# The second tile's products ahead of the third tile's transposes, in the maps of the mean and in the last projection

## Chip, cores and metric

The kernel runs on one core of one Trainium2 chip. The metric is device microseconds for one execution. The kernel before takes 3393.33 us, the median of three runs (3391.39 to 3394.57).

## What is computed

Four graph layers follow one another on 3327 nodes with 512 features, all with the same adjacency matrix. Each layer's output is added to its input and normalised row by row:

```python
x = _layernorm(x + _L0_gnn_ref(x, adj, W, a))                 # attention, 8 heads of 64
x = _layernorm(x + _L1_gnn_ref(x, adj, W_nb, b_nb, W_line, b_line, 64))  # mean of up to 64 neighbours
x = _layernorm(x + _L2_gnn_ref(x, adj, W, a))                 # attention, 8 heads of 64, then elu
x = _layernorm(x + _L3_gnn_ref(x, adj, W, a))                 # attention, 4 heads of 128, then elu
```

The mean layer maps the mean of a node's neighbours with `W_nb`, and the node itself with `W_line`; each map has a bias and a leaky relu, and the two are added. An attention layer begins with a projection, `Wh = x @ W`, from which the scores of the heads are taken as well:

```python
Wh = (h @ W).reshape(n, H, D)
s1 = jnp.einsum('nhd,hd->nh', Wh, a1)
s2 = jnp.einsum('nhd,hd->nh', Wh, a2)
```

## The kernel before

The 3327 rows are padded to 26 tiles of 128 (`NT`). The stages follow one another: projection and attention of layer 0; the maps of the mean (first part of `sage`, lines 712 to 775), that is both linear maps applied to the rows of layer 0; the sums over the kept neighbours together with the projection of layer 2 (second part of `sage`); attention of layer 2; the projection of layer 3 (first part of `third`, lines 897 to 942); attention of layer 3 and the output.

The two stages that are edited have the same form. A tile's row of work is:

- *Finish* the layer before (`finish`, `finish_steps`, `norm_rows`), two tiles at a time. The attention's sums `h` are loaded from memory, and the residual rows `xr` with them; VectorE divides (L181) and adds (L197, or L194 and L195 around an exponential L186 on ScalarE), takes statistics (L152, L153), ScalarE takes the root (L154), VectorE the reciprocal and the shift (L155, L158), and ScalarE normalises the rows in place (L161).
- *Transpose* the tile: four TensorE transposes into PSUM (L724 in `step1`, L261 in `project1`) and one copy to SBUF on ScalarE, `xT` (L726, L262). In the last projection VectorE sums `xT` as well (L263).
- *Products* of the transposed tile. In the maps these are `step2`: four matmuls with `wn` into `pz` (L732), four with `wl` into `pi` (L735). The profile lists each of these fp32 matmuls as two, so a tile has 16. ScalarE casts `pz` to bf16 (L736), VectorE subtracts (L738), ScalarE casts the remainder (L739), VectorE makes the third piece (L741) and finishes the map of the node itself (L744, L745, L746); two stores go out on SP's queue (L742, L747). In the last projection they are `project2`: eight matmuls of 260 columns into two banks (L271, 16 in the profile), an exponential (L272) and two small copies (L275) on ScalarE, two multiplications on VectorE (L277), and one store on SP (L283).

The loop runs one tile behind itself: the products of a tile are kept in `pend` and issued after the transposes of the next tile, so that the copy of the transposed tile is covered. For tiles 0, 1, 2 the order on TensorE is thus transposes 0, transposes 1, products 0, transposes 2, products 1, transposes 3, products 2. Tiles 0 and 1 (`first`) were already finished by the stage before; the loop handles two tiles in each pass (`t0`), and asks for the next two when it has transposed the first of a pair.

What sets the order: `tc.manual_schedule` at the top keeps TensorE in the order in which the program issues its instructions. The other engines' instructions are put in order by the scheduler, except those that are marked `keep_in_program_order`. Each engine works through its own queue in that order. PSUM tiles of the stage (`pt`, and `pz`, `pi`, or the two banks `pw`) have two buffers each. In the last projection, after the products of tile 13, `prepare` transposes the scores of the first half (L312), copies them (L314) and stores them; thirteen small transposes in groups of four share two PSUM buffers.

Of the kernel before, what the change touches and what calls it, by code (L numbers as in the profile page):

```python
# [32 lines left out]
def kernel(  # L33
# [94 lines left out]
    def store_tile(dst, src, t, eng):  # L128
        if dst.shape[0] == N and t == NT - 1 and LAST < P:
            for a, z in _row_pieces(LAST):  # L130
                eng.dma_start(out=dst[t * P + a:t * P + z, :], in_=src[a:z, :])
        else:
            eng.dma_start(out=dst[t * P:(t + 1) * P, :], in_=src)

    def load_w(pool, src, name, eng=None):
        t = pool.tile([P, FC, src.shape[1]], F32, name=name)
        (eng or nc.scalar).dma_start(out=t, in_=src.rearrange("(c p) m -> p c m", p=P))
        return t


    def load_wide(t, src, eng):
        for e in range(2):
            eng.dma_start(out=t[:, :, e, :FW], in_=src[:, e * FW:(e + 1) * FW].rearrange("(c p) m -> p c m", p=P))
# [61 lines left out]
    def finish(*a):  # L205
        ys, steps = finish_steps(*a)
        for f in steps:
            f()
        return ys
# [476 lines left out]
    def sage(first, first_pool, xin, prev, nxt, wsrc, dst):  # L686
# [3 lines left out]
        with tc.tile_pool(name="sg_z", bufs=1, reuse_waits="tile") as zp, \  # L690
# [17 lines left out]
            def zs(t, c):  # L708
                return zs_[t // HALF][:, t % HALF, c, :]

            zd = dram.tile([NP, F], BF, name="zd")
            with tc.tile_pool(name="sa_w", bufs=1, reuse_waits="tile") as wp, \
                    tc.tile_pool(name="sa", bufs=2, reuse_waits="tile") as fp, \
                    tc.tile_pool(name="sa_t", bufs=2, reuse_waits="tile") as sp, \
                    tc.tile_pool(name="sa_ps", bufs=2, space=PSUM, reuse_waits="tile") as ps:
                wn = load_w(wp, wnT, "wn", nc.gpsimd)
                wl = load_w(wp, wlT, "wl", nc.gpsimd)
                blb = wp.tile([P, F], F32, name="blb")
                nc.gpsimd.dma_start(out=blb, in_=bl.to_broadcast([P, F]))

                def step1(xt):
                    pt = ps.tile([P, FC, P], F32, name="pt")
                    for c in range(FC):
                        nc.tensor.transpose(pt[:, c, :], xt[:, c * P:(c + 1) * P], ident)  # L724
                    xT = sp.tile([P, FC, P], F32, name="xT")
                    nc.scalar.copy(xT, pt)  # L726
                    return xT

                def step2(xt, xT, t):
                    pz = ps.tile([P, F], F32, name="pz")  # L730
                    for c in range(FC):
                        nc.tensor.matmul(pz, xT[:, c, :], wn[:, c, :], start=c == 0, stop=c == FC - 1)  # L732
                    pi = ps.tile([P, F], F32, name="pi")
                    for c in range(FC):
                        nc.tensor.matmul(pi, xT[:, c, :], wl[:, c, :], start=c == 0, stop=c == FC - 1)  # L735
                    nc.scalar.copy(zs(t, 0), pz)  # L736
                    r1 = sp.tile([P, F], F32, name="r1")
                    nc.vector.tensor_tensor(r1, pz, zs(t, 0), op=ALU.subtract)  # L738
                    nc.scalar.copy(zs(t, 1), r1)  # L739
                    z3 = sp.tile([P, F], BF, name="z3")  # L740
                    nc.vector.tensor_tensor(z3, r1, zs(t, 1), op=ALU.subtract)  # L741
                    nc.sync.dma_start(out=zd[t * P:(t + 1) * P, :], in_=z3)  # L742
                    xi = sp.tile([P, F], F32, name="xi")
                    nc.vector.tensor_tensor(xi, pi, blb, op=ALU.add)  # L744
                    nc.vector.scalar_tensor_tensor(xi, xi, 0.01, xi, op0=ALU.mult, op1=ALU.max)  # L745
                    nc.vector.tensor_tensor(xi, xi, xt, op=ALU.add)  # L746
                    nc.sync.dma_start(out=xid[t * P:(t + 1) * P, :], in_=xi)  # L747


                cr = fp.tile([NT, P], BF, name="cr", bufs=1)  # L750
                nc.sync.dma_start(out=cr, in_=ctd[NT:NT + 1, :].rearrange("o (t p) -> (o t) p", p=P))
                cnt = zp.tile([P, 3, NT], F32, name="cnt")
                pend = None
                ahead = first
                for t0 in range(0, NT, 2):
                    ys = ahead
                    if t0 in (4, 8):
                        prev.late.pop(0)(fp)
                    if t0 == 8:
                        cf = fp.tile([NT, P], F32, name="cf", bufs=1)  # L760
                        nc.scalar.copy(cf, cr)
                        pt = ps.tile([P, FC, P], F32, name="pt")
                        cb = pt[:, 0, :NT]
                        nc.tensor.transpose(cb, cf, ident[:NT, :NT])
                        nc.vector.tensor_scalar(cnt[:, 0, :], cb, NEIGHBOURS, 1.0, op0=ALU.min, op1=ALU.max)
                        nc.vector.reciprocal(cnt[:, 1, :], cnt[:, 0, :])
                        nc.vector.tensor_scalar(cnt[:, 2, :], cb, 0.0, None, op0=ALU.is_gt)
                    for s, y in enumerate(ys):
                        xT = step1(y)
                        if s == 0 and t0 + 2 < NT:  # L770
                            ahead = finish(fp, xin, prev, t0 + 2, 2, 6, nc.sync if t0 else nc.gpsimd)
                        if pend:
                            step2(*pend)
                        pend = (y, xT, t0 + s)
                step2(*pend)
            first_pool.close()

            with tc.tile_pool(name="sb_w", bufs=1, reuse_waits="tile") as wp, \
# [8 lines left out]
                wsb = wp.tile([P, FC, 2, FW + nxt.H], F32, name="wsb")  # L787
# [60 lines left out]
                for b in range(len(blocks)):  # L848
                    t0, i0 = blocks[b]
# [42 lines left out]
    def third(first):  # L892
        with tc.tile_pool(name="col3", bufs=1) as cp, tc.tile_pool(name="at_r3", bufs=2, reuse_waits="tile") as rp:
# [3 lines left out]
            with tc.tile_pool(name="p_w", bufs=1, reuse_waits="tile") as wp, \  # L897
                    tc.tile_pool(name="p", bufs=3, reuse_waits="tile") as pp, \
                    tc.tile_pool(name="p_f", bufs=2, reuse_waits="tile") as fp, \
                    tc.tile_pool(name="p_ps", bufs=2, space=PSUM, reuse_waits="tile") as ps:  # L900
                wsb = wp.tile([P, FC, 2, FW + L3.H], F32, name="wsb")

                def bank(e):
                    return ps.tile([P, 512], F32, name=f"pw{e}")


                pend = None
                ahead = first
                groups = []

                def load_group(t0):
                    if t0 < NT:
                        groups.append(finish_steps(fp, x2, L2, t0, 2, 10, nc.gpsimd if t0 < 4 else nc.sync, 6,
                                                    pinned=t0 == 2))
                        groups[-1][1].pop(0)()

                load_group(2)
                load_wide(wsb, w3, nc.gpsimd)
                nc.vector.tensor_copy(wsb[:, :, :, FW:], wa[3].rearrange("p c (e h) -> p c e h", e=2))
                load_group(4)  # L920
                for t0 in range(0, NT, 2):
                    ys = ahead
                    if t0 in (4, 8):
                        L2.late.pop(0)(fp)
                    load_group(t0 + 6)
                    for s, y in enumerate(ys):
                        t = t0 + s
                        store_tile(x3, y, t, nc.sync)
                        xT = L3.project1(pp, ps, y, t)
                        if s == 0 and groups:  # L930
                            ahead, steps = groups.pop(0)
                            for f in steps:
                                f()
                        if pend:
                            L3.project2(pp, bank, wsb, *pend)
                        pend = (xT, t)
                        if t == HALF + 1:
                            L3.prepare(pp, 0)
                            L3.first_rows = L3.rows(rp, 0, 0)
                            L3.cut(pp, 0)  # L940
                L3.project2(pp, bank, wsb, *pend)
                L3.mean(pp, bank, wsb)

# [129 lines left out]
    L0, L2, L3 = Layer(0, 8, False), Layer(2, 8, True), Layer(3, 4, True)  # L1073
# [3 lines left out]
    with tc.tile_pool(name="col0", bufs=1) as cp, tc.tile_pool(name="raw", bufs=2) as rawp, \  # L1077
# [4 lines left out]
        with tc.tile_pool(name="p_w", bufs=1, reuse_waits="tile") as wp, \  # L1082
# [37 lines left out]
            wsb = wp.tile([P, FC, 2, FW + L0.H], F32, name="wsb")  # L1120
# [3 lines left out]
            pend = (xT, 0)  # L1124
            for t in range(1, NT):
                xT = L0.project1(pp, ps, load(t), t)
                L0.project2(pp, bank, wsb, *pend)
                pend = (xT, t)
# [96 lines left out]
```

## Time and profile before

| | us |
|---|---|
| median of three runs | 3393.33 |
| the profiled execution | 3389.15 |
| its span | 3387.4 |
| TensorE busy | 3251.2 |
| VectorE busy | 2687.5 |
| ScalarE busy | 2354.6 |
| maps of the mean: first transposes of a tile to the last product | 960.2 to 1168.2 |
| last projection: first transposes to the last product | 2555.9 to 2684.1 |

The mean granted clock of TensorE was 0.985 of full speed.

How to read the lines shown below. PE is TensorE's matmuls, PEld its weight loads, DVE VectorE, ACT ScalarE, POOL GpSimd, SP SyncE. In the timeline, each line gives the start and the duration in us, the engine, the line of the program, the operation, what it writes and reads, how many instructions are merged, and in brackets how long the engine had been idle before and which instruction released it. A line of the waits says who waited for whom, in us in total, how often, and the longest. A line of the stretches gives its bounds and length in us; then the busy time and the number of instructions of PE, PEld, DVE, ACT and POOL; then the granted clock, the DMA share and GB/s.

### The profile page before, as it was taken

What the parts mean: (1) busy time and instruction counts of PE and PEld (TensorE: products, weight loads), DVE (VectorE), ACT (ScalarE), POOL (GpSimd) and SP (SyncE); (2) the same over time, 40 slices, a digit from 0 to 9 for tenths busy, and PEclk for the clock granted to TensorE, in tenths of its full rate; (3) what the DMA queues carried; (4) which work ended last, traced back from release to release, by engine and by line L of the source; (5) the groups of instructions that cost most, each with busy time, mean ns of one, the idle gap of its engine ahead of it and who ended that gap; (6) DMA issues with size and microseconds to landing.
All of it is one profiled execution on the core that took longest, in us unless ns stands there. A gap on an engine that the chain in (4) does not pass through costs nothing.

```text
span 3387.4 us, 47182 instructions
## 1 busy us (share of the span) xinstructions
PE 3251.2 (96%) x18476; PEld 1626.4 (48%) x18476; DVE 2687.5 (79%) x2619; ACT 2354.6 (70%) x2143; POOL 239.8 (7%) x389
## 2 busy tenths in 40 slices
PE   8899999999979999999989999999998999999997
PEld 7634344444434445545544444444446754455453
DVE  5799999999967544444449999999998766668887
ACT  2398998999953333333338999999997655558986
POOL 3100000000010011111110000000002000010110
PEclk9999999999999999999999999999998999999998
DMA  9644111110143343333320111111117411122211
GB/s 368 222 124 127 49 49 38 55 49 28 44 123 125 122 117 84 91 85 87 80 77 20 47 48 50 51 48 47 35 31 241 152 41 42 41 51 80 94 42 49
DMA packets 288014, 284.29 MB, mean 84 GB/s; under 512 B 107492, under 2 KB 223534, under 8 KB 287791
## 3 DMA queue, kind: packets, MB, share of 16 engines
q1 hardware_dynamic: 254063, 170.62, 16.6%
q0 software_dynamic: 28208, 102.96, 9.5%
q10 hardware_dynamic: 5520, 7.69, 0.7%
q8 instruction: 146, 2.39, 0.3%
q14 instruction: 77, 0.63, 0.1%
HBM read 212.01 MB, written 69.17 MB: 83 GB/s over the span
## 4 chain that ended last, share of the span: by engine, by line
PE 85%; DVE 5%; DMA 4%; ACT 3%; issue 2%; SPq 0%; ACTq 0%; DVEq 0%; POOL 0%; POOLq 0%
PE po L428 52%; PE acc L859 12%; PE pd L380 7%; PE pw L271 5%; DVE t L405 3%; PE pz L732 3%; DMA raw<-in_adjT_dram 3%; PE pi L735 3%; ACT y L408 1%; PE pt L456 1%; PE pk L819 1%; DMA h<-hd 0%; PE pa L1108 0%; PE pt L724 0%; PE pct L664 0%
## 5 line engine op out<-in xcount | busy, mean ns | idle before, releaser
L405 DVE SCALAR_TENSOR_TENSOR t<-rb,qc,mask 128x1664 f32<-128x1664 f32 x1040 | 1960.3, 1954 | 169.4 <-PE po L428 147.3
L408 ACT ACTIVATE y<-t,bi,sc 128x1664 fp8e4<-128x1664 f32 x1040 | 1769.5, 1766 | 310.4 <-PE pd L380 292.7
L428 PE MATMUL po<-t,vj 128*64 128x448 f32 (+3 forms) x8320 | 1909.6, 521 | 22.1 <-DVE t L405 19.6
L428 PEld LDWEIGHTS po<-t,vj 128*64 128x64 f32 (+1 forms) x8320 | 838.9, 148 | 970.6 <-issue 704.0
L859 PE MATMUL acc<-zs,kt 128*128 128x512 bf16 x1352 | 401.1, 380 | 0.0
L271 PE MATMUL pw<-wsb,xT 128*128 128x264 f32 (+1 forms) x1248 | 302.2, 397 | 15.2 <-DVE vt L277 12.0
L859 PEld LDWEIGHTS <-kt 128*128 128x128 fp8e4 x2002 | 196.1, 98 | 242.1 <-issue 7.7
L811 ACT CAST pk<-cy 128x512 f32<-128x512 bf16 x169 | 99.0, 588 | 277.4 <-DVE kt L823 266.3
L271 PEld LDWEIGHTS pw<-wsb,xT 128*128 128x128 f32 x1248 | 241.1, 197 | 60.7 <-ACT xT L262 10.8
L380 PE MATMUL pd<-y,sden 128*32 128x448 fp8e4 (+1 forms) x4160 | 259.5, 342 | 10.4 <-ACT y L408 10.4
L859 PE MATMUL acc<-zl,kt 128*128 128x512 bf16 x650 | 246.5, 379 | 0.0
L380 PEld LDWEIGHTS <-sden 128*32 128x32 bf16 x4160 | 117.5, 96 | 162.5 <-issue 139.8
L823 DVE SCALAR_TENSOR_TENSOR kt<-pk,mask 128x512 fp8e4<-128x512 f32 x169 | 116.1, 688 | 94.0 <-PE pk L819 94.0
L277 DVE TENSOR_TENSOR vt<-pw,dc 128x256 f32<-128x256 f32 x156 | 59.0, 418 | 148.2 <-ACT dc L272 143.7
L359 POOL DMA_DIRECT2D rb<-r x40 | 21.3, 532 | 1670.4 <-DVE t L405 1652.2
L275 ACT COPY rc<-pw 128x8 f32<-128x8 f32 (+1 forms) x78 | 12.6, 162 | 156.6 <-PE pw L271 154.1
L831 DVE SCALAR_TENSOR_TENSOR y<-acc,cnt,bnb 128x512 f32<-128x512 f32 x26 | 19.5, 751 | 97.7 <-PE acc L859 90.3
L732 PE MATMUL pz<-wn,xT 128*128 128x512 f32 x208 | 94.9, 600 | 1.7 <-ACT xT L726 1.7
L700 POOL DMA_DIRECT2D cy<-ctd x91 | 67.9, 746 | 385.1 <-ACT pk L811 312.6
L735 PE MATMUL pi<-wl,xT 128*128 128x512 f32 x208 | 93.5, 592 | 0.0
L634 DVE TENSOR_SCALAR mask<-raw 128x832 fp8e4<-128x832 int32 (+2 forms) x90 | 54.8, 614 | 38.9 <-DMA raw<-in_adjT_dram 38.5
L154 ACT ACT_TABLE_LOAD x45 | 57.7, 1283 | 37.0 <-DVE mv L153 36.4
(187 smaller groups left out, 1699.3 us busy)
## 6 DMA issues: line engine op xcount, KB each, us to landing
vj<-v SPq DMA_DIRECT2D x312, 128.0 KB
rb<-r POOLq DMA_DIRECT2D x40, 832.0 KB, 4.8
raw<-in_adjT_dram SPq DMA_DIRECT2D x67, 416.0 KB
cy<-ctd POOLq DMA_DIRECT2D x78, 256.0 KB, 4.0
h<-hd SPq DMA_DIRECT2D x61, 256.0 KB
v<-vt SPq DMA_DIRECT2D x50, 256.0 KB
hd<-hb SPq DMA_DIRECT2D x48, 256.0 KB
xr<-x POOLq DMA_DIRECT2D x45, 256.0 KB, 3.1
```

What stands on the lines that cost most here:

```text
L271: nc.tensor.matmul(pw[e][:, :FW + H], xT[:, c, :], wsb[:, c, e, :], start=c == 0, stop=c == FC - 1)
L277: nc.vector.tensor_tensor(vt[:, hs, :], pw[e][:, :FW].rearrange("p (h d) -> p h d", d=D), self.dc[:, t, hs].rearrange("p (h e) -> p h e", e=1)
L380: nc.tensor.matmul(pd[c][32 * kk:32 * kk + 32, :w_], lhsT, rhs, start=(kk, c) not in seen, skip_group_check=final is not None, stop=last a ...
L405: nc.vector.scalar_tensor_tensor(t, rb[k], self.qc[:, j, h:h + 1], mask[:, j, i0:i0 + IW], op0=ALU.max, op1=ALU.mult)
L408: nc.scalar.activation(y, t, AF.Sigmoid, bias=self.bi[:, j, h:h + 1], scale=self.sc[:, j, h:h + 1], saturate=False)
L428: nc.tensor.matmul(po[c][k * D:(k + 1) * D, :z - a_], vj[:, j % 2, k * D:(k + 1) * D], ts[k][:, a_:z], start=j == 0, stop=j == NT - 1)
L700: nc.gpsimd.dma_start(out=cy[:, :n, :], in_=ctd[t:t + n, b * GW:(b + 1) * GW] .rearrange("(o t) i -> o t i", o=1).to_broadcast([P, n, GW]))
L732: nc.tensor.matmul(pz, xT[:, c, :], wn[:, c, :], start=c == 0, stop=c == FC - 1)
L735: nc.tensor.matmul(pi, xT[:, c, :], wl[:, c, :], start=c == 0, stop=c == FC - 1)
L811: nc.scalar.copy(pks[k % 2], carry[b, t // 4 * 4][:, t % 4:t % 4 + 2, :])
L823: nc.vector.scalar_tensor_tensor(kt, pk, NEIGHBOURS, mask[:, t:t + 2, i0:i0 + GW], op0=ALU.is_le, op1=ALU.mult, saturate=False)
L859: nc.tensor.matmul(acc, kts[t][:, s * P:(s + 1) * P], zs(t, c) if c < 2 else zl[:, t, :], start=t == 0 and c == 0, stop=t == NT - 1 and c ...
```

## The change

In both loops, at the end of the first pass (tiles 0 and 1), the pending products are issued and `pend` is cleared. The next pass then finds nothing pending when it has transposed tile 2, and goes on to the transposes of tile 3 before it issues the products of tile 2. From the transposes of tile 4 on, the order is as before.

```diff
                         if pend:
                             step2(*pend)
                         pend = (y, xT, t0 + s)
+                    if t0 == 0:
+
+                        step2(*pend)
+                        pend = None
                 step2(*pend)
...
                             L3.cut(pp, 0)
+                    if t0 == 0:
+
+                        L3.project2(pp, bank, wsb, *pend)
+                        pend = None
                 L3.project2(pp, bank, wsb, *pend)
                 L3.mean(pp, bank, wsb)
```

On TensorE the order for tiles 0 to 3 becomes transposes 0, transposes 1, products 0, products 1, transposes 2, transposes 3, products 2, products 3 after the transposes of tile 4. No instruction is added to TensorE or taken away. The built program differs from the one before as follows. In the maps of the mean the order on VectorE and ScalarE differs for the instructions of tiles 1 to 7 alone, and the queues of SP and GpSimd hold the same transfers in the same places. In the last projection VectorE, ScalarE and SP are ordered differently from tile 1 to near the end of the stage, ScalarE has two more table loads, and GpSimd is as before. Elsewhere the two programs have the same order.

## Prediction

> In what follows T*n* is the group of four transposes of tile n (L724 in the maps of the mean, L261 in the last projection), P*n* its products (L732 and L735, or L271), y*n* its normalised rows (the L161 activation), xT*n* the copy of the transposed tile out of PSUM (L726 or L262).
>
> **What bounds the kernel now.** I read the page first, then the waits of PE in the two stages that are edited, then the timeline of both, engine by engine.
>
> ```profile
> span 3387.4 us, 47182 instructions
> PE 3251.2 (96%) x18476; PEld 1626.4 (48%) x18476; DVE 2687.5 (79%) x2619; ACT 2354.6 (70%) x2143; POOL 239.8 (7%) x389
> ```
>
> PE is busy for 96% of the span, so a hole on PE is worth its length if PE is what the stage ends on. The waits of PE from 940 to 1170 us have one large entry, and those of the last projection (2535 to 2700 us) another:
>
> ```profile
> PE pt L724 <- ACT h L161: 13.8, 1, 13.8
> ```
>
> ```profile
> PE pt L261 <- ACT h L161: 11.8, 2, 8.5
> ```
>
> Both are PE waiting for the third tile's rows. The timeline shows what stands behind that wait:
>
> ```profile
> 966.53 3.60 PE L735 MATMUL pi<-wl,xT 128*128 128x512 f32 x8
> ...
> 983.10 1.52 ACT L161 ACTIVATE h<-h,rs 128x512 f32<-128x512 f32 x2 [1.62 <-issue]
> ...
> 983.97 1.11 PE L724 MATMUL pt<-ident,h 128*128 128x128 f32 x4 [13.84 <-ACT h L161]
> 984.14 1.28 DVE L152 BATCH_NORM_STATS2 st<-h 128x6 f32<-128x512 f32 x2
> ...
> 984.87 4.83 PE L732 MATMUL pz<-wn,xT 128*128 128x512 f32 x8
> ...
> 993.41 3.60 PE L732 MATMUL pz<-wn,xT 128*128 128x512 f32 x8
> ```
>
> P0 ends at 970.1; P1 could run from there (its xT was copied by 963.4), but T2 is ahead of it in the queue and waits until 983.97. P2 starts only at 993.41. From then on PE never waits before the stage ends, as the stretches show (busy, then instructions; PE 20.00 of 20.00 in each stretch from 1000 to 1160):
>
> ```profile
> 1100.00:1120.00 20.00, 20.00 (x57) 9.41 (x56) 14.06 (x26) 6.71 (x12) 1.14 (x3) 1.00 0.39 128
> ```
>
> In the last projection the same hole is smaller, and PE is not alone:
>
> ```profile
> 2559.27 5.79 PE L271 MATMUL pw<-wsb,xT 128*128 128x260 f32 x14 [0.30 <-DMA wsb<-in_w_dram]
> 2573.51 1.12 PE L261 MATMUL pt<-ident,h 128*128 128x128 f32 x4 [8.46 <-ACT h L161]
> 2574.42 5.42 PE L271 MATMUL pw<-wsb,xT 128*128 128x260 f32 x16
> ...
> 2580.12 3.67 PE L271 MATMUL pw<-wsb,xT 128*128 128x260 f32 x16
> ...
> 2601.26 3.77 PE L271 MATMUL pw<-wsb,xT 128*128 128x260 f32 x16 [0.98 <-ACT xT L262]
> ...
> 2618.61 3.75 PE L271 MATMUL pw<-wsb,xT 128*128 128x260 f32 x16 [1.30 <-ACT xT L262]
> ...
> 2634.75 0.75 PE L312 MATMUL pr<-ident,rc 128*4 128x128 f32 x5 [3.64 <-ACT rr L314]
> ```
>
> PE waits for ACT again at 2601, 2618 and 2634; DVE is busy for 18.3, 19.1 and 19.9 us of the three 20 us stretches from 2590 to 2650. Only from 2650 on does PE run without a gap.
>
> [...] P1 stood behind T2 for 13.8 us with its operands there. [...] the four transposes after the hole took 1.11 us against 0.60 later, the eight pz products 4.83 against 3.60. [...] The loads here average 1283 ns[...] (a load starts at 2574.19, its activation at 2575.48), so I use 1.28.
>
> **The change, first place.** P1 goes in front of T2. What moves with it: its 16 PE records, two ACT casts (L736, L739), five DVE operations and two stores on SP. The order of the built program shows POOL unchanged and SP's queue here with the same stores in the same places. DVE and ACT are unchanged up to y2 and y3, so y2 still comes at about 983.9. Step by step, with the durations above:
> - P1 runs 970.1 to 977.0, inside the hole. T2 starts at 983.97 as before, T3 follows when y3 is out (984.6), at half rate, and ends at 986.2.
> - ACT now holds, between y3 and the copy xT2: cast zs (0.57), cast of the remainder (0.62), the root for tiles 4 and 5 (0.29). The remainder needs a DVE subtraction that is queued behind the two statistics of 984.14 to 985.4, so it is ready at 986.0; the cast ends at 986.7, the root at 986.9, xT2 (0.58) at 987.45. P2 starts at 987.5 instead of 993.41: 5.9 us earlier.
> - Clock. Before, the granted clock was 0.90 over 984 to 1000 and 1.00 after: half rate for 3.2 us, to about 987.3, so the next window would end at 990.7. Now PE idles again from 986.2 to 987.5, and the window to 987.3 is only two thirds full, of transposes. In the last projection T0, T1 and P0, with a 1 us gap between, ran at half rate for all of their 9 us (granted clock 0.66 over 2550 to 2565), so I take it that this window doesn't lift the throttle and the next does: P2 runs at half rate until 990.7 and loses half of 3.2 us, 1.6. Bounds: 0 if it lifts, 3.3 if one more window is needed.
> - P2 takes 6.87 (993.41 to the next tile's transposes at 1000.28), so it ends at 987.5 + 6.9 + 1.6 = 996.0 against 1000.28: **4.3 us** earlier.
> - What is late next: y4 and y5. DVE now does P1's five operations among the steps of tiles 4 to 7; walking its queue at 0.6 us an operation, y4 is out at 990.4 and T4 wants it at 996. Later tiles' loads wait for buffers that P2's and later outputs free, so they move with PE. PE stays full to the stage's end, and the next stage waits for its last stores: the 4.3 us pass on.
>
> **Second place.** P1 here is 16 records, 3.5 us (2580.12 to 2583.63), 5.4 after a hole. With it go on ACT two small copies, one exponential and its table load; on DVE two multiplications; on SP one store of v, now ahead of three small loads of the denominators and four tile loads. That store waits for DVE (about 2575.2), so the tile loads go out at about 2577.6 instead of 2576.84; the operation that waited for one at 2579.96 now stands about 9 us later in DVE's queue, which hides it.
> - P1 runs 2565.1 to 2568.6 at full rate. Its exponential comes ahead of y2 on ACT, but the load and it (1.45 us from 2570.1) fit before the 2572.5 at which DVE releases y2. T2 starts at 2573.51 as before, T3 ends at 2575.7, P2 runs from there, half of it slow, to 2580.35 against 2583.63: 3.3 us earlier.
> - Then the gain is given back. On ACT, y4 and y5 now stand behind P2's copy, a table load and its exponential, and these wait for the end of P2: 2580.35 + 0.15 + 1.28 + 0.15 + 0.75 gives y4, and so T4, at 2582.6 against 2583.63. Only 1.0 us is left.
> - Behind that, the scheduler has ordered DVE and ACT anew down to the stage's end, with products earlier and normalisation later, and two more table loads in all. I walked both queues by the same durations: PE is ahead by 2.3 us at P7 (the 0.98 wait goes), by 0.5 at T10, behind by 1.9 at T12 (y12 waits 2.25 us on PE), and about even when P13 ends (2630.1). In the preparation that follows, the rr copies stand ahead of two normalisations on ACT instead of behind them, and the 3.64 us wait shrinks by 1.6. After it PE runs from a backlog. I take **1.4 us** gained; since a walk of 60 us through coupled queues is easily off by 2 to 3, the bounds are 2 lost and 3.5 gained (all of P1).
>
> Sum: 4.3 + 1.4 = 5.7 us. The profiled execution took 3389.15 (span 3387.4 and 1.75 around it), 4.2 below the median of the runs, 3393.33. Taken from the median: **3387.6**, 0.17% less.
>
> **Rivals.**
> - *The whole of P1 is won twice*: the clock lifts at once and the projection's queues don't bind. 6.9 + 3.5 = 10.4 us, 3382.9. For it: PE at 96%. Against: the copy xT2 behind ACT's queue, and DVE at 19 of 20.
> - *The projection gives back more than it wins*: 4.3 less about 3, so 1.3 us, 3392.0. For it: DVE and ACT nearly full there, two more table loads. Against: the backlog of tiles after 2650.
> - *Slower*: in the projection each pair of tiles from 4 to 14 is normalised behind an exponential that waits for the products before it. If all six pairs stall PE by the 2.25 us that I find for one, that is 13.5 us; less 3.5 and 4.3, 5.7 us slower, 3399.0. It decides from 1.3 us a pair. Against: the walk finds such a stall at three pairs, and old stalls go.
> - *The change does nothing*: excluded, since PE's order in the built program differs in just these two places.
>
> **Numbers.** Forecast 0.48, whole gain 0.24, given back 0.21, slower 0.07. The range is 3382.5 to 3393.5: it takes in the first three but for a tail of the second. A measurement here tells about 0.2% (6.8 us) from no change. Faster by more: the 0.24 and a quarter of the forecast, 0.36. Slower by more: half of the slower case, 0.04. Within: 0.60.
>
> **What would show it.** Right: P1 directly behind P0 in both places; P2 about 5.9 us earlier in the maps, slow for its first 3 us; PE then full; T4 of the projection waiting for y4 by about 2 us; the end of the projection's products 5 to 6 us earlier on the whole. Wrong: P2 at full rate from its start, a wait of PE in the maps after 996, or waits for L161 at most pairs of tiles in the projection.

## The result, and the profile after

| | before | after |
|---|---|---|
| median, us (runs) | 3390.98 (8) | 3381.8 (8) |
| lowest to highest | 3386.04 to 3394.57 | 3380.32 to 3385.6 |
| the profiled execution | 3389.15 | 3385.6 |

After takes 0.9974 of before, with a 95% interval of 0.9964 to 0.9985: 5 to 12 us less. The forecast was 3387.6. The median of before, 3393.33 over three runs, came down to 3390.98 over eight, so 2.35 of the 5.8 us between forecast and result are in the base; the other 3.5 are gain that the forecast didn't have (9.2 instead of 5.7).

The two profiled executions differ by only 3.5 us: that of after is the slowest of its eight. A single pair of profiles would have led to a wrong sum, so below each stage is compared on its own.

The first lines of the page of after, then the waits of PE in the stretches of the two stages:

```profile
span 3383.9 us, 47143 instructions
PE 3250.5 (96%) x18424; PEld 1626.0 (48%) x18476; DVE 2685.5 (79%) x2619; ACT 2356.1 (70%) x2145; POOL 239.4 (7%) x389
```

```profile
PE pt L724 <- ACT h L161: 7.0, 1, 7.0
...
PE pz L732 <- ACT xT L726: 1.8, 2, 1.4
```

```profile
PE pt L261 <- ACT h L161: 10.3, 4, 6.1
...
PE pr L312 <- ACT rr L314: 2.4, 2, 1.2
```

The page counts 18424 instructions on PE against 18476 before. No instruction was taken away: some matmul records are missing from this trace, and the weight loads are 18476 in both.

In the maps 13.8 us of waiting became 7.0, and 1.4 of a new wait, for the copy xT2. In the projection the two sums for normalised rows (10.3 us here, 11.8 before) can't be compared as they stand: the 11.8 hold 3.4 us at T0, the start of the stage, which the profile of after puts down to a DMA. From T2 on it is 8.5 us at one place before and 10.3 at four places after, so this wait grew. What shrank are waits that the change doesn't touch: those of P7 and P11 for xT (0.98 and 1.30 us in before) are gone, and that for the copies rr in the preparation fell from a longest of 3.6 us to 1.2.

The maps on PE:

```profile
969.19 3.60 PE L732 MATMUL pz<-wn,xT 128*128 128x512 f32 x8
972.62 3.60 PE L735 MATMUL pi<-wl,xT 128*128 128x512 f32 x8
983.17 1.97 PE L724 MATMUL pt<-ident,h 128*128 128x128 f32 x8 [6.96 <-ACT h L161]
986.59 5.17 PE L732 MATMUL pz<-wn,xT 128*128 128x512 f32 x8 [1.44 <-ACT xT L726]
```

P1 runs right behind P0. T2 and T3 share a line (8 instructions). Where TensorE's granted clock is 0.50, the text speaks of half rate: in this profile and in that of before the records of the maps' products then start 0.85 us apart, and 0.43 us at full rate (medians). This profile enters the stage 0.80 us earlier than before; with that added, P2 starts at 987.39 (forecast 987.5). Its first products are at half rate for a part of their time, 5.17 us instead of 3.60.

The last projection on PE:

```profile
2557.71 7.80 PE L271 MATMUL pw<-wsb,xT 128*128 128x260 f32 x30 [0.21 <-DMA wsb<-in_w_dram]
2571.62 1.97 PE L261 MATMUL pt<-ident,h 128*128 128x128 f32 x8 [6.11 <-ACT h L161]
2573.41 5.42 PE L271 MATMUL pw<-wsb,xT 128*128 128x260 f32 x16
2580.83 0.66 PE L261 MATMUL pt<-ident,h 128*128 128x128 f32 x4 [2.00 <-ACT h L161]
...
2606.26 0.66 PE L261 MATMUL pt<-ident,h 128*128 128x128 f32 x4 [1.54 <-ACT h L161]
...
2615.05 0.66 PE L261 MATMUL pt<-ident,h 128*128 128x128 f32 x4 [0.68 <-ACT h L161]
...
2627.63 1.04 PE L312 MATMUL pr<-ident,rc 128*4 128x128 f32 x8 [0.53 <-ACT rc L275]
2629.88 0.75 PE L312 MATMUL pr<-ident,rc 128*4 128x128 f32 x5 [1.21 <-ACT rr L314]
```

P0 and P1 follow one another (30 instructions in one line), T2 still waits for y2, and T4 (2580.83), T10 (2606.26) and T12 (2615.05) now wait for their rows. The two groups of L312 are the preparation, and the wait of 1.21 between them stands where before had 3.64.

### The profile page after: what moved, and what is told of

Same layout as the page of the kernel before. It is cut to its first block, busy times and chain, and to the rows that moved or that the text cites. A ratio compares the mean times of both kernels' runs of the same rounds, so it can differ in the third digit from the quotient of the medians.

```text
span 3383.9 us, 47143 instructions
## 1 busy us (share of the span) xinstructions
PE 3250.5 (96%) x18424; PEld 1626.0 (48%) x18476; DVE 2685.5 (79%) x2619; ACT 2356.1 (70%) x2145; POOL 239.4 (7%) x389
## 4 chain that ended last, share of the span: by engine, by line
PE 82%; DVE 5%; DMA 4%; issue 4%; ACT 3%; POOL 0%; SPq 0%; ACTq 0%; POOLq 0%; DVEq 0%
PE po L428 50%; PE acc L863 12%; PE pd L380 7%; PE pw L271 4%; DVE t L405 2%; PE pz L732 2%; PE pi L735 2%; DMA raw<-in_adjT_dram 2%; ACT y L408 1%; PE pk L823 1%; PE pt L456 1%; DMA h<-hd 1%; PE pa L1116 0%; DVE st L152 0%; DVE vt L277 0%
## 5 line engine op out<-in xcount | busy, mean ns | idle before, releaser
L863 PE MATMUL acc<-zs,kt 128*128 128x512 bf16 x1312 | 393.8, 381 | 2.3 <-issue 0.4
```

Source lines behind the costliest of these rows:

```text
L863: nc.tensor.matmul(acc, kts[t][:, s * P:(s + 1) * P], zs(t, c) if c < 2 else zl[:, t, :], start=t == 0 and c == 0, stop=t == NT - 1 and c ...
```

## Where the profiled pair differs

Taking the same VectorE and ScalarE instructions in both traces and subtracting their starts gives how far after is ahead, along the span. Each step is where this number moves:

| stretch | after gains, us |
|---|---|
| before the maps | 0.8 |
| maps (T2 to the end) | 4.4 |
| start of the sums over neighbours, 1165 to 1180 | -0.7 |
| a preparation in that stage, near 1490 | -1.7 |
| near 1750 and 1795, end of the sums | -1.4 |
| last projection | 4.15 |
| 3103: an L186 activation waits 4.1 us for a load | -1.7 |
| the end | -0.4 |
| sum | 3.5 |

The two stages that are edited gain 8.6 us together. The rest is not the edited code. To see which of it comes again, the kernels below were profiled too.

## Experiments

Four times serve to compare the last projection between profiles, all read from starts on PE: from T0 to T2, from T2 to the first L312, from there to the second group of L312, and from there to the mean's products (L293). The last column is their sum. For the maps it is the time from T2 to the last pz.

| kernel | T0 to T2 | to L312 | to second L312 | to L293 | T0 to L293 | maps |
|---|---|---|---|---|---|---|
| before | 17.63 | 56.56 | 4.68 | 49.63 | 128.50 | 180.36 |
| before_again | 16.85 | 56.45 | 4.53 | 50.83 | 128.65 | 180.17 |
| maps_only | 18.05 | 56.26 | 4.52 | 48.94 | 127.76 | 176.04 |
| proj_only | 17.62 | 55.70 | 2.25 | 48.85 | 124.41 | 181.72 |
| after | 17.20 | 56.02 | 2.25 | 48.86 | 124.33 | 175.91 |
| after_again | 17.76 | 55.65 | 2.25 | 48.84 | 124.50 | 175.86 |
| norm45_first | 17.25 | 56.47 | 2.25 | 48.86 | 124.83 | 175.94 |
| rr_late | 17.06 | 56.01 | 5.60 | 50.49 | 129.16 | 176.16 |
| rr_late_timed | 18.03 | 55.57 | 5.61 | 50.20 | 129.41 | 177.46 |
| rr_early | 17.07 | 56.34 | 1.27 | 49.49 | 124.17 | 180.32 |
| maps_and_rr | 17.28 | 56.15 | 1.27 | 49.48 | 124.19 | 175.89 |
| maps_copy_first | 16.86 | 55.98 | 2.25 | 48.86 | 123.95 | 175.58 |
| maps_busy | 17.87 | 55.82 | 2.24 | 48.85 | 124.78 | 175.72 |
| maps_busy_copy | 17.08 | 55.81 | 2.25 | 48.84 | 123.98 | 173.64 |

Theory of the forecast: the maps give 4.3, the projection 1.4. Rival after the result: the projection gives about 4. A second rival came up with the traces: what the projection gains isn't won by the moved products but by the copies rr, which the scheduler put elsewhere in ScalarE's queue.

### The two edits, each alone, and both kernels again

maps_only leaves out the second edit, that of the last projection:

```diff
-                    if t0 == 0:
-
-                        L3.project2(pp, bank, wsb, *pend)
-                        pend = None
```

> The first edit alone (maps of the mean). Both theories agree here: by the time that the stretch to the end of the maps lost in the profile, 4.4 to 4.5 us less than before, so about 3386.5. From P2 of the maps on, everything stands 4.45 us earlier than before against the entry of the stage, and at the projection the order and the waits are those of before (a wait of about 8.5 us before T2, about 3.6 us before the second group of L312). Theory 'chance': the median can still move by some 2 us either way, since half-rate windows fall differently from run to run. If the projection's edit is worth nothing, this run already shows all of the 9 us.

proj_only leaves out the first, that of the maps:

```diff
-                    if t0 == 0:
-
-                        step2(*pend)
-                        pend = None
```

> The second edit alone (last projection). Theory 'undersized': the projection gains about 4.2 us between its entry and its end, as the profile after shows: about 2.5 us of moved work and 1.7 us because P14 is no longer at half rate; median about 3386.8. Theory 'as forecast': the projection gains 1.4 us, median 3389.6, and the rest of the 9.2 us between the medians is run to run variation; then the stretch from T2 to the mean's products shrinks by 1 to 2 us in this profile.

after_again and before_again have no edit.

> The changed kernel unaltered, for a second profile and a median on the same chip. If both gains are of the change's own and add up: about 3382 (8.6 less than before), the maps 4.4 and the projection about 4 us shorter again, and half-rate windows outside of the two stages at other places than in the first profile. If the projection's part was chance: P14 at half rate again here, and the projection 1 to 3 us shorter only.

> The kernel before unaltered, for a second profile and as a measure of what the comparison can tell: 3391, ratio 1.000 within 0.0005. If the half rate of P14 (5.36 us instead of 3.67) follows from the 3.6 us wait before it, it is there again; if it was chance, it may be missing, and the projection is then 1.7 us shorter.

| kernel | median, us (runs) | ratio to before | 95% interval |
|---|---|---|---|
| maps_only | 3386.21 (21) | 0.9989 | 0.9982 to 0.9995 |
| proj_only | 3386.21 (21) | 0.9986 | 0.9979 to 0.9992 |
| after_again | 3382.3 (12) | 0.9977 | 0.9968 to 0.9985 |
| before_again | 3391.37 (13) | 0.9999 | 0.9991 to 1.0008 |

Before itself took 3389.98 here (56 runs), so by these ratios the edits give 3.7 and 4.7 us alone, and 7.8 together (9.2 in the first comparison). The ratio is an estimate of its own and not the quotient of the two medians, so equal medians can have different ratios; the two edits can't be told apart by them. Within the intervals they add up. The maps gain 4.3 us, as forecast: 180.3 us in before and before_again, 175.9 in maps_only, after and after_again. Two other profiles of the table have one more half-rate window in the maps: proj_only, whose maps are the old ones (181.72), and rr_late_timed, whose maps are the new ones (177.46). The projection gains 3.9 us in the mean, 3.3 to 4.3 from profile to profile, and never 1.4: the forecast's theory falls on this term. In before_again the half rate of P14 came again (its products took 5.71 us, 5.36 in before), in maps_only it was missing (3.67 us) after the same wait of 3.5 us, and the projection was then 0.8 us shorter: a part of the 3.9 depends on how such a window falls.

The table of stretches says where the 3.9 us are, as means of the three profiles with the old order (before, before_again, maps_only) and the three with the edit (proj_only, after, after_again): 0.0 up to T2, 0.6 from T2 to the first L312, 2.3 in the wait between the two groups, 0.95 behind it. So 3.3 of the 3.9 appear at and behind the wait for rr, 50 us away from the products that were moved. The 0.95 is a mean of 0.8, 2.0 and 0.1: it comes from the half rate of P14 in before and before_again.

### The copies rr, put late and put early

In the profile of before ScalarE does this while PE waits:

```profile
2629.65 1.28 ACT L154 ACT_TABLE_LOAD   x1
2630.95 0.29 ACT L154 ACTIVATE rs<-mv,eps 128x2 f32<-128x2 f32 x1
2631.26 1.28 ACT L272 ACT_TABLE_LOAD   x1
2632.56 0.17 ACT L272 ACTIVATE dc<-pw 128x4 f32<-128x4 f32 x1
2632.63 1.51 ACT L161 ACTIVATE h<-h,rs 128x512 f32<-128x512 f32 x2
...
2634.13 1.04 ACT L314 COPY rr<-pr 4x512 f32<-4x512 f32 x2
```

and in that of after:

```profile
2627.77 1.28 ACT L154 ACT_TABLE_LOAD   x1
2629.07 0.29 ACT L154 ACTIVATE rs<-mv,eps 128x2 f32<-128x2 f32 x1
2629.27 1.03 ACT L314 COPY rr<-pr 4x512 f32<-4x512 f32 x2
2630.90 0.81 ACT L161 ACTIVATE h<-h,rs 128x512 f32<-128x512 f32 x1 [0.59 <-DVE rs L158]
```

The eight transposes that the copies read are finished by 2631.1 before and 2628.7 after. Before, the copies stand in the queue behind a table load, an exponential and the normalisation of tiles 16 and 17, 3 us of work; after, right behind the root. ScalarE took them in their turn: copies that could have run at 2631.1 ran at 2634.13. In the traces of before and after, the computing instructions of ScalarE (2143 and 2145) and VectorE (2619 in both) start in the order of the built program, compared by line, and so do the matmuls of PE and the transfers issued by SP and GpSimd.

rr_late leaves both edits in place and puts the first copy back behind that normalisation (`norm_ins[0]` is its last L161, and `issue_after` queues what follows behind it on ScalarE). rr_late_timed is the same kernel:

```diff
-                nc.scalar.copy(rr[:, :n * P], pr[:H, :n * P])
+                if behind is not None and s0 == 0:
+                    with tc.issue_after(behind):
+                        nc.scalar.copy(rr[:, :n * P], pr[:H, :n * P])
+                else:
+                    nc.scalar.copy(rr[:, :n * P], pr[:H, :n * P])
...
-                            L3.prepare(pp, 0)
+                            L3.prepare(pp, 0, behind=norm_ins[0])
```

> The changed kernel, with the first copy rr of the preparation (L314) queued on ScalarE behind the normalisation of tiles 16 and 17, as before; the moved products stay moved. Theory 'the copies' place': most of the projection's 3.9 us comes from rr standing ahead of that normalisation, so the wait before the second group of L312 grows from 1.2 to about 3.5 us, and from T2 to L293 takes 109 to 110 us instead of 106.9. Theory 'the moved products': the wait may grow but the stage is paced elsewhere, 106.5 to 107.5 us.

> The kernel of rr_late (both edits in place, the first copy rr queued behind the normalisation of tiles 16 and 17), now for its median. Theory 'the copies' place': the projection's whole gain is lost and what stays is the maps', so about as fast as maps_only (3386, ratio 0.9989), and the stretch from T2 to L293 takes 109.5 to 112 us again. Theory 'the moved products': 3382 to 3383 (ratio 0.9976).

rr_early moves no products at all; it only traces the normalisation of tiles 16 and 17 after the preparation and queues it behind the second copy (VectorE's part of `norm_rows` for these two tiles comes later with it). maps_and_rr is the same on top of the first edit:

```diff
                             ahead, steps = groups.pop(0)
+                            last = steps.pop() if t == HALF + 1 else None
                             for f in steps:
...
                             L3.prepare(pp, 0)
+                            with tc.issue_after(L3.second_rr):
+                                last()
```

> The kernel before (no products moved in either place), with the normalisation of tiles 16 and 17 queued on ScalarE behind the first two copies rr of the preparation. Theory 'the copies' place': the wait of 3.5 to 3.6 us before the second group of L312 falls to about 1.2 us, P14 runs at full rate, and from T2 to L293 takes 107.5 to 108.5 us instead of 109.7 to 111.8, without the change. Theory 'the moved products': it stays at 109.5 or more.

> The first edit (maps of the mean) as in the change, but the last projection with its products where they were before; instead, the normalisation of tiles 16 and 17 is queued on ScalarE behind the first two copies rr, as in rr_early. Theory 'the copies' place': the projection gains 4 us this way too, so the whole is as fast as the changed kernel, 3382 (ratio 0.9975), and a direct comparison of the medians can't tell the two apart. Theory 'the moved products': 3384 to 3386, since their part of the projection's gain is missing.

PE in rr_late (two lines up in the numbering, so L314 is the transpose of the scores):

```profile
2625.40 1.03 PE L314 MATMUL pr<-ident,rc 128*4 128x128 f32 x8 [0.37 <-ACT rc L277]
2631.00 1.23 PE L314 MATMUL pr<-ident,rc 128*4 128x128 f32 x5 [4.57 <-ACT rr L318]
2632.03 1.06 PE L263 MATMUL pt<-ident,h 128*128 128x128 f32 x4
2632.88 5.36 PE L273 MATMUL pw<-wsb,xT 128*128 128x260 f32 x16
```

and in rr_early:

```profile
2627.53 1.04 PE L312 MATMUL pr<-ident,rc 128*4 128x128 f32 x8
2628.79 0.75 PE L312 MATMUL pr<-ident,rc 128*4 128x128 f32 x5 [0.23 <-ACT rr L314]
2629.38 0.60 PE L261 MATMUL pt<-ident,h 128*128 128x128 f32 x4
2629.81 3.67 PE L271 MATMUL pw<-wsb,xT 128*128 128x260 f32 x16
```

With the copies late, the wait is 4.57 us, P14 (the last line) runs at half rate again, and the projection takes 129.2 and 129.4 us, although its products are moved. The median is 3388.7 us, a ratio of 0.9992 (0.9984 to 1.0000): what stays is at most the maps' part. The forced order is a little worse than the old one (the scheduler put a table load and an exponential L188 in between too), which can be why it overshoots by 1 us. With the copies early and nothing moved, the projection takes 124.2 us, as with the edit; maps_and_rr takes 124.2 us there too. Its median, 3383.59 us, lies between the numbers of the two theories (3382, and 3384 to 3386), and its ratio, 0.998 (0.9973 to 0.9987), can't be told from that of the changed kernel; the times of the stage decide, and not the median. They support theory "the copies' place" from both sides (one profile each of rr_early and maps_and_rr, two with the copies late): in the last projection moving P1 is worth 0.6 us up to the preparation, and the copies' place 3.3, of which 0.95 depend on how half-rate windows fall.

### Why the moved products gain so little there

norm45_first takes away the wait at T4; P2's work on ScalarE is queued behind the last L161 of tiles 4 and 5:

```diff
-                        if pend:
-                            L3.project2(pp, bank, wsb, *pend)
+                        if pend and t == 3:
+                            with tc.issue_after(norm_ins[0]):
+                                L3.project2(pp, bank, wsb, *pend)
+                        elif pend:
+                            L3.project2(pp, bank, wsb, *pend)
```

> The changed kernel, with the exponential and copies of P2 of the last projection queued on ScalarE behind the normalisation of tiles 4 and 5, so that T4 need not wait for P2 (2.00 us in the changed kernel). From the start of T2 to the mean's products (L293) the changed kernel takes 106.8 to 107.1 us. Theory 'queues bind': the wait at T4 goes, but the time comes back at T10 and T12, where ScalarE and VectorE are late; the first L312 and L293 come within 1 us of where they were (106 to 107.5). Theory 'holes on TensorE add up': L293 comes 2 us earlier, 104.9.

```profile
2577.16 0.60 PE L263 MATMUL pt<-ident,h 128*128 128x128 f32 x4
...
2595.57 0.90 PE L263 MATMUL pt<-ident,h 128*128 128x128 f32 x4 [2.46 <-ACT h L163]
2596.26 5.16 PE L273 MATMUL pw<-wsb,xT 128*128 128x260 f32 x16
```

T4 (first line) no longer waits, and neither does T10, but T8 waits 2.46 us for its rows, and the products behind it run at half rate (5.16 us instead of 3.67). The first L312 comes 56.47 us after T2, no earlier than in before (56.4): a hole closed at one tile opened at a later one. That the chain of normalised rows through VectorE and ScalarE paces this stretch, and not the holes on PE, fits this; it rests on one profile, in which about 1.5 us of the loss are the half rate.

### The copy and the half rate in the maps

maps_copy_first traces everything of P1 behind its cast zs after T2, and queues it on ScalarE behind the copy xT2:

```diff
                         xT = step1(y)
+                        if t0 == 2 and s == 0:
+                            with tc.issue_after(copied[0]):
+                                step2(*first_pend, parts=(1,))
...
-                        step2(*pend)
+                        step2(*pend, parts=(0,))
+                        first_pend = pend
                         pend = None
```

> The changed kernel, with the copy xT2 of the maps queued on ScalarE ahead of the cast of P1's remainder, which now follows it. In the changed kernel PE waits 1.44 us for that copy. Theory 'the copy's place in the queue': xT2 is copied 1.0 to 1.3 us earlier, P2 starts that much earlier, and the end of the maps comes 0.6 (all of the gain at half rate) to 1.3 us earlier against T2. Rival: the copy waits for the transposes themselves at half rate, and P2 moves by less than 0.4 us.

It gained 0.33 us. P2 came 3.05 us after the start of T2 instead of 3.42. That is the rival's size, but not for the rival's reason: the copy still stood behind the root for tiles 4 and 5, which waited 1.1 us for VectorE.

```profile
987.60 0.29 ACT L154 ACTIVATE rs<-mv,eps 128x2 f32<-128x2 f32 x1 [1.11 <-DVE mv L153]
987.80 0.57 ACT L726 COPY xT<-pt 128x512 f32<-128x512 f32 x1
```

maps_busy adds work whose result nobody uses, in the hole before T2, and queues the root and the normalisation of tiles 4 and 5 behind xT2; maps_busy_copy has this and the edit of maps_copy_first. Only the added matmuls are shown:

```diff
                         pend = None
+                        warm = qp.tile([P, F], F32, name="warm", tag="q")
+                        for k in range(6):
+                            nc.tensor.matmul(warm, ident, wn[:, k % FC, :], start=True, stop=True)
```

> The changed kernel with six more matmuls of 128x512 (results unused) behind P1 in the maps, in the hole before T2, to keep TensorE from the half rate; the root and normalisation of tiles 4 and 5 queued behind the copy xT2. Theory 'half rate costs 1.6 us', as forecast: T2, T3 and P2 run at full rate (eight products pz 3.60 instead of 5.17 us), and from T2 to the last pz takes 1.6 to 2 us less than 175.9, if T2 itself starts no later. Rival: the half rate comes anyway or ScalarE's order delays P4, and the stretch is within 0.5 us of 175.9.

> The changed kernel with both edits of the maps: the six unused matmuls in the hole, and the copy xT2 ahead of the cast of P1's remainder and of the root for tiles 4 and 5. If both effects add up: from T2 to the last pz about 173.5 us instead of 175.9 (1.6 from the clock, 0.4 to 0.9 from the copy), median about 3379.5, 2.5 less than the changed kernel. If VectorE's and ScalarE's queues take it back: within 1 us of the changed kernel.

maps_busy was a miss: T2 and T3 ran at full rate (1.36 us for both), but P2's first products took 5.16 us all the same, after two waits of 1.84 and 1.87 us around the transposes, and the stretch is 175.72. In maps_busy_copy the second wait is gone:

```profile
976.36 5.31 PE L800 MATMUL warm<-wn,ident 128*128 128x512 f32 x12
984.08 1.36 PE L724 MATMUL pt<-ident,h 128*128 128x128 f32 x8 [2.41 <-ACT h L161]
985.74 3.70 PE L736 MATMUL pz<-wn,xT 128*128 128x512 f32 x8 [0.30 <-ACT xT L726]
```

P2 runs at full rate (3.70 instead of 5.17), and the maps take 173.64 us, 2.3 less than after. With 3376.59 us (5 runs, 3375.73 to 3379.26), it has the lowest median of all kernels here, and its slowest run is below the fastest of both sets of runs of the changed kernel (3379.66). It ran on another chip than after_again, and its ratio to before, 0.9964 (0.9951 to 0.9978), overlaps with those of the changed kernel. In this profile the half rate that the forecast counted at 1.6 us was won back, 1.5 us in the pz line alone, with the unused matmuls and the early copy together. Of the 5 to 6 us between its median and those of the changed kernel, 2.3 are in the maps, and up to 1.7 can be the window of the next part, which its profile lacks; the rest is not accounted for.

### A half-rate window near 1490 us

Near 1490 us, in the stage of the sums, another preparation makes PE wait for a copy rr. The stretch behind that wait, from 1495 to 1500 in before and from 1490 to 1495 in after (busy and instructions of PE, PEld, DVE, ACT and POOL, then the granted clock):

```profile
1495.00:1500.00 5.00, 4.73 (x23) 2.22 (x24) 0.79 (x2) 1.39 (x3) 0.75 (x1) 1.00 0.03 7
```

```profile
1490.00:1495.00 5.00, 3.75 (x11) 1.52 (x13) 0.69 (x1) 1.25 (x3) 0.00 (x0) 0.66 0.03 7
```

In after the clock was at half for 3.4 us, which costs the 1.7 us of the table above. The wait ahead of it was 2.2 to 2.4 us in eight profiles, all with the edit of the maps, and seven of them show the window; it was 1.8 in six (before, before_again, proj_only, rr_early, maps_copy_first, maps_busy_copy), and none does. So in most of these profiles the maps' gain is partly given back 330 us later. The traces show what PE waits for there: rr has one buffer in this stage, and the second copy waits until the store of the first has landed, 1.9 us in the six profiles (1.88 in before), 2.2 to 2.5 in the eight (2.21 in after). Why that store takes longer was not tried, so that the edit causes it is not shown.

## Why the prediction was wrong

- *P1 into the hole of the maps, P2 at 987.5, 1.6 us of half rate, 4.3 us gained*: right, each of them. Measured: 987.39; half rate up to 990.4 on before's clock (forecast 990.7, that is the end of half rate in before, 987.35, and one more window; the windows in before last 3.41 us); 4.3 us in the means of the profiles. That the partly idle window before it would not bring full rate back was an estimate; in the profiles half rate followed 126 of 126 half-rate windows with more than 0.55 us idle (last section). The bound "3.3 if one more window is needed" came true in one profile, rr_late_timed, where P2's first products took 6.72 us.
- *PE stays full to the stage's end*: right. After P2 no wait for L161 is left in the stage. *The 4.3 us pass on*: not wholly in most profiles, because of the window near 1490, which the forecast didn't look for.
- *Projection, "both are PE waiting for the third tile's rows"*: a misreading. Of the 11.8 us only 8.5 are at T2; the other 3.4 are at T0. The walk starts from T2 at 2573.51 and is not touched by it.
- *T4 waits for y4, only 1.0 us is left*: right (the sum for y4 comes to 2582.7, and not 2582.6). T4 waited 2.00 us and starts 9.21 us after T2 instead of 10.12: 0.9.
- *PE ahead by 2.3 us at P7 and 0.5 at T10, behind by 1.9 at T12, y12 waits 2.25, about even when P13 ends*: right up to T10 (2.26 and 0.66, against the start of T2), too pessimistic from there. T12 waits 0.68 and is behind by 0.23, and the first L312 comes 0.6 us earlier.
- *The wait for rr shrinks by 1.6*: the mechanism was right, the size was 2.3.
- *"After it PE runs from a backlog"*, counted at nothing: wrong. The 3.5 us wait had put P14 at half rate in two of three profiles; without it the rest of the stage is 0.95 us shorter in the mean.
- **The failing term** is therefore the "1.4 us" for the last projection: it measured 3.9. Its parts were 0.6, 2.3 and 0.95. That is more than the upper bound, 3.5, which took all of P1 as the most that could be won; most of the gain came from another engine's queue. The forecast had found the copies' new place but treated it as one correction in a walk of 60 us, when it is the one that decides the stage.
- *The base*: the median of three runs was 1.6 to 3.4 us above those of the four larger sets of runs of the same kernel (8 to 56 runs). Together with the term above this puts the result 0.7 us under the low end of the range.
- *Rivals*: "the whole of P1 is won twice" named 3382.9, close to the result, but for reasons that did not occur: the clock didn't lift in the maps, and P1's move in the projection won 0.6 us and not 3.5. "Gives back more" and "slower" are excluded: the stalls at pairs are 2.0, 1.5 and 0.7 us and are paid for.
- *What stays open*: 4.3 and 3.9 make 8.2 us, less up to 1.7 for the window near 1490; the two comparisons gave 7.8 (5 to 11) and 9.2 (5 to 12). They can't say whether all of the 1.7 is lost in a typical run.

## What to carry to other kernels

A change of order on one engine reaches the others through the scheduler: compare every queue of the built program, and price each place where a waiting engine's releaser has moved, since that can be worth more than the step that was meant. To find out which of them acts, pin the one without the other, from both sides. And compare profiles by stage, not by span: single runs of the kernel before lay 8.5 us apart among eight and 12.8 among 56, as much as the effect or more, while the edited stages repeated within some tenths of a microsecond, half-rate windows apart.

## What the runs showed of the hardware

Half rate came in stretches of 3.41 us or a multiple of it in all 14 profiles, up to 17.07 us (the end of the execution left out), at other places from run to run. Within one profile all these stretches start on one grid of 3.41 us, to 0.01 us. In before, for example, TensorE's granted clock was 0.50 from 973.69 to 987.35 us, four steps of the grid, and from 1751.93 us for one step. One step of the grid is a window here. A window needn't be wholly idle for half rate to follow: in before_again (below) one with 2.67 us of idle time was enough.

How much idle time goes with it can be counted. For each window of the grid, from 100 to 3340 us of the 14 profiles, the time without a matmul record was added up and compared with the granted clock of the next window. The ends of matmuls are modelled by the profile, so these times are not exact.

| window | idle on PE, us | at half rate next |
|---|---|---|
| at full rate | more than 2.0 | 126 of 126 |
| at full rate | 1.6 to 2.0 | 28 of 83 |
| at full rate | less than 1.6 | 10 of 12786 |
| at half rate | more than 0.55 | 126 of 126 |
| at half rate | 0.55 or less | 1 of 165 |

The ten exceptions all lie near 573 us, behind windows without any idle time; their cause is open. In these profiles, whether a wait costs a window thus depends on how it falls on the grid. Ahead of P14 two windows that follow one another, first in before_again, then in maps_only (busy time and instructions of PE come first, the granted clock third from the end):

```profile
2630.33:2633.74 3.41, 0.74 (x7) 0.35 (x5) 3.41 (x16) 3.37 (x6) 0.54 (x1) 1.00 0.47 162
2633.74:2637.15 3.41, 2.58 (x11) 2.15 (x12) 3.41 (x15) 2.41 (x8) 0.54 (x1) 0.50 0.81 211
```

```profile
2630.97:2634.39 3.42, 1.67 (x12) 1.38 (x13) 3.42 (x14) 3.22 (x8) 0.64 (x2) 1.00 0.68 178
2634.39:2637.80 3.41, 3.41 (x19) 2.97 (x18) 3.41 (x8) 2.00 (x4) 0.00 (x0) 1.00 0.84 290
```

The wait was 3.5 us in both. In before_again 2.67 us of idle time fell into one window, in maps_only 1.73 and 1.74 into two. Near 1490 us the seven profiles with the half-rate window have 2.16 to 2.45 us in one window, the eighth has 1.78 and 0.81 in two, and the six others at most 1.88. In maps_busy 2.10 us of the two waits fell into one window, in maps_busy_copy 1.37 and 1.39 into two; so the waits around the transposes, and how they fell on the grid, decided there. The transposes are counted as busy in all this: they are 1.36 of the 2.02 us that PE was busy in the second window of maps_busy_copy, and full rate followed. Without them that window would have 2.75 us idle, and above 2.0 half rate followed every time.
